# A fused attention and expert kernel: k's copies on ACT, and one batch's choice of experts put behind another's norm

## The chip, the cores and the metric

The kernel runs on one core of a Trainium2 chip. The metric is the device time of one execution in microseconds (us). The engines are PE (TensorE: matrix products and transposes), DVE (VectorE), ACT (ScalarE), POOL (GpSimd) and SP (SyncE, which here only issues DMAs). Each engine has a queue of its own that it works off in order; a semaphore wait at its head holds everything behind it.

## What is computed

Two layers with residuals on x, which is 4 batches of 512 tokens of 256 numbers, all in 32-bit floats:

```
x = x + attn(layernorm(x)) ; x = x + ffn(layernorm(x))

attn(x):  q = k = elu(x @ Wqk + bqk)            # 16 heads of 16
          v = silu(x @ Wv + bv) ; u = silu(x @ Wu + bu)
          kv = k.T @ v (per head) ; out = q @ kv
          out = layernorm(out, ln_g, ln_b) * u
          return out @ Wo + bo

ffn(x):   logits = x @ gate                     # 8 experts
          two best experts per token, softmax over the two
          h = silu(x @ w0[e]) * (x @ w1[e])     # 256 -> 512
          return sum over the two of weight * (h @ wo[e])
```

## The kernel before

**Attention.** `attention(b)` is a Python generator for one batch. Between its `yield`s lie twelve stages, which are numbered here from 0:

- 0: first norm (DVE, and L280 on ACT for odd tiles); 1: transposes of the normed x (L292)
- 2: q and k, which are the same array (L317, exp L322, L323, L324)
- 3: v (L346, L351, L358) and, for batches 0 to 2, u (`project`, L334, L338)
- 4: k's rows: PE transposes them into two PSUM banks (L391), and each bank of 128x512 is copied to SBUF (L394)
- 5: kv (L421, masked at L429); 6: out (L442, copied by L446) and, for batch 3, u
- 7: second norm, `layernorm(..., "2")`; 8: its transposes (L292), scale (L457) and product with u (L461)
- 9: output projection (L469), the residual sum (L473) and the store of the sum to the output (L476, issued by ACT)
- 10: choice of experts (L498 to L520): the two best of eight, third norm, exp for the softmax (L516)
- 11: each token's place in its expert's region, by products with constant matrices (L524, L526), then eight indirect DMAs on POOL that write the rows to `xg` in DRAM (L539)

The norm takes statistics (L252, L253) of four tiles, then ten small dependent DVE steps (L255 to L272), then scales the tiles (L284 on DVE, L280 on ACT).

**Order.** The driver loop counts `at` from 0. Batch b runs stage `at - begin[b]`, with `begin = [0, 4, 8, 12]`, and within one `at` later batches come first. So batch 2 (B - 2) has its stages 9, 10 and 11 at 17, 18 and 19, where batch 3 has its stages 5, 6 and 7.

**Experts.** The rows in `xg` are worked on in blocks of 128 of one expert. After batch 1's stage 11, at 16, `plan` finds nine blocks that are full of the rows of batches 0 and 1 already (`early`). Each block is advanced in a pipeline (`advance`): `fetch` (L715, on SP) loads its rows; `turn` transposes them (L726, copied by L729) and copies two of its expert's weights to a fixed place (L741, ACT and DVE); two half layers (L759 or, for blocks shared by two experts, L767) with silu (L843) and product (L778); `finish` (L798), scale (L809) and an indirect DMA on POOL that adds the rows to the output (L819). `ready` holds the blocks, with `None` where an `at` passes without one: the first early block is fetched at 18, the second at 20, and then one at each `at`.

Blocks that need all batches (`last`, `full`, `second`) come behind the early ones, once batch 3's counts are known.

**What else sets the order.** The tiles' framework schedules: the calls' order is a priority, and an instruction that it takes to be ready goes ahead of one that waits, so that the order on an engine is fixed at compile time but is not the program's. PSUM has eight banks, handed out in turn by `bank`. The last eight weights, `w2` (L174, on SP, called for at 21), are loaded into slots of `arena` that held k and token tiles, so each load waits for the slot's last reader; three of them wait for batch 3's L442 and for the transposes L292 of batches 2 and 3.

Of the kernel before, what the change touches and what calls it, by code (L numbers as in the profile page):

```python
# [32 lines left out]
def kernel(  # L33
# [32 lines left out]
    nc = tc.nc  # L66
    B, N, E = x.shape
    NE, _, M = w0.shape
# [9 lines left out]
    EARLY = 2 * N * TOPK // P - NE + 1  # L78
# [17 lines left out]
    def bank(shape, name, n=1):  # L96

        at = (used[0] + used[0] % n) % BANKS
        used[0] = (at + n) % BANKS
        if n == 2:  # L100
            return banks[:, at : at + 2, 0 : shape[2]]
        tile_ = banks[:, at, 0 : math.prod(shape[1:])]
        if len(shape) == 3:
            tile_ = tile_.rearrange("p (a b) -> p a b", a=shape[1])
        return tile_
# [9 lines left out]
    def att(tag):  # L115

        i = turns[tag] % COUNT[tag]
        turns[tag] += 1
        if tag == "kv":
            return arena[:, AT[tag], bass.ts(i, E)]  # L120
        return arena[:, AT[tag] + i, :]
# [50 lines left out]
    def load_w2():  # L172
        for e in range(NE):
            nc.sync.dma_start(  # L174
                out=arena[:, e, :].rearrange("p (c d) -> p c d", c=MC),
                in_=w2[e].rearrange("(c p) d -> p c d", p=P),
            )
# [121 lines left out]
    def attention(b):  # L299
# [14 lines left out]
        for c in range(EC):  # L314
            ps = bank([P, N], f"qp_{b}_{c}")
            for k in range(EC):
                nc.tensor.matmul(  # L317
                    ps, lhsT=wqk_sb[:, k, bass.ts(c, P)], rhs=xT[:, k, :],
# [23 lines left out]
        for t0 in range(0, NT, 2):  # L342
            ps = bank([P, 2, E + NE], f"vp_{b}_{t0}", 2)
# [18 lines left out]
        if b == 0:  # L362

            ps = bank([P, NE], "gate_sum")
            for k in range(EC):
                nc.tensor.matmul(
                    ps, lhsT=ones, rhs=wv_sb[:, k, E:], start=(k == 0), stop=(k == EC - 1)
# [9 lines left out]
            ps = bank([P, EC, E], "woTp")  # L377
# [8 lines left out]
        kn = att("tok").rearrange("p (t e) -> p t e", t=NT)  # L386
        for t0 in range(0, NT, 2):
            ps = bank([P, 2, E], f"knp_{b}_{t0}")
            for t in range(t0, t0 + 2):
                for c in range(EC):  # L390
                    nc.tensor.transpose(  # L391
                        ps[:, t - t0, bass.ts(c, P)], kT[:, c, bass.ts(t, P)], ident
                    )
            nc.vector.tensor_copy(kn[:, t0 : t0 + 2, :], ps)  # L394
        if b == 0:

            ps = bank([P, EC + 1, NE], "wog")
# [18 lines left out]
        ps = bank([P, EC, HALF], f"kvp_{b}")  # L416
# [21 lines left out]
        for t0 in range(0, NT, 2):  # L438
            ps = bank([P, 2, E], f"op_{b}_{t0}")
# [25 lines left out]
        for t0 in range(0, NT, 2):  # L465
            ps = bank([P, 2, E + NE], f"ap_{b}_{t0}", 2)
# [26 lines left out]
        ps = x1[:, :, E:]  # L493
# [35 lines left out]
        at = small.tile(four, F32, tag="at", name=f"at_{b}")  # L529
# [15 lines left out]
    def total():  # L545

        tot = bank([P, NE], "tot")
        nc.tensor.matmul(tot, lhsT=ones, rhs=state["count"], start=True, stop=True)
        return tot
# [33 lines left out]
    def tmp(shape, what, name):  # L583
        return small.tile(shape, F32, tag=what, name=f"{what}_{name}", bufs=1)

    def upto_each(new, name):

        sq = tmp([1, NE, NE], "sq", name)
        nc.vector.tensor_tensor(
            sq, new.unsqueeze(1).to_broadcast([1, NE, NE]), upto[0:1], ALU.mult  # L590
        )
        cum = tmp([1, NE], "cum", name)
        nc.vector.tensor_reduce(cum, sq, AX.X, ALU.add)
        return cum

    def listed(cum, base, n, name):


        nc.vector.tensor_tensor(
            step[:, 0 : NE - 1], base[:, 1:NE], base[:, 0 : NE - 1], ALU.subtract  # L600
        )

        grid = [1, n, NE]
        behind = tmp(grid, "behind", name)
        nc.vector.tensor_tensor(
            behind, ordinal[:, 0:n, :], cum.unsqueeze(1).to_broadcast(grid), ALU.is_ge
        )
        which = tmp([1, n], "which", name)
        nc.vector.tensor_reduce(which, behind, AX.X, ALU.add)
        nc.vector.tensor_tensor(  # L610
            behind, behind, step.unsqueeze(1).to_broadcast(grid), ALU.mult
        )
        first = tmp([1, n], "first", name)
        nc.vector.tensor_reduce(first, behind, AX.X, ALU.add)
        nc.vector.scalar_tensor_tensor(
            first, first, base[:, 0:1], rows[:, 0:n], ALU.add, ALU.add
        )
        table = const.tile([1, 2, n], I32, name=f"table_{name}")
        nc.vector.tensor_scalar(table[:, 0, :], first, float(NE * REG), None, ALU.min)
        nc.vector.tensor_scalar(table[:, 1, :], which, float(NE - 1), float(OW), ALU.min, ALU.mult)  # L620
        return table
# [36 lines left out]
    def plan(tot, n, b, name):  # L658

        vec = [1, NE]
        c = tmp(vec, "c", name)
        nc.vector.tensor_tensor(c, tot[0:1, :], region[0:1], ALU.subtract)
        full = [1, NE, T // P]
        over = tmp(full, "over", name)
        nc.vector.tensor_tensor(
            over, c.unsqueeze(2).to_broadcast(full), ends, ALU.is_ge
        )
        new = tmp(vec, "new", name)  # L670
        nc.vector.tensor_reduce(new, over, AX.X, ALU.add)
        if b == B - 1:
            nc.vector.tensor_tensor(new, new, done, ALU.subtract)

        cum = upto_each(new, name)
        cumex = tmp(vec, "cumex", name)
        nc.vector.tensor_tensor(cumex, cum, new, ALU.subtract)

        base = tmp(vec, "base", name)
        if b == B - 1:  # L680
            nc.vector.tensor_tensor(base, done, cumex, ALU.subtract)
            nc.vector.scalar_tensor_tensor(base, base, float(P), region[0:1], ALU.mult, ALU.add)
        else:
            nc.vector.scalar_tensor_tensor(base, cumex, -float(P), region[0:1], ALU.mult, ALU.add)
        table = listed(cum, base, n, name)
        if b == B - 1:
            state["found"] = const.tile([1, 1], I32, name="found")
            state["cum"] = const.tile(vec, F32, name="cum_full")
            nc.vector.tensor_copy(state["cum"], cum)
        else:  # L690
            nc.vector.tensor_scalar(done, cumex, -1.0, float(n), ALU.mult, ALU.add)
            nc.vector.scalar_tensor_tensor(done, done, 0.0, new, ALU.max, ALU.min)
        return [
            (f"{name}_{j}", b, None, [table[0:1, 0, j : j + 1]], [table[0:1, 1, j : j + 1]])
            for j in range(n)
        ]
# [160 lines left out]
    STAGES = 12  # L857
    W2_AT = 9
    begin = [0, 4, 8, 12]
    running = [attention(b) for b in range(B)]  # L860
    ready = []
    for at in range(max(begin) + STAGES + 1):
        for b in reversed(range(B)):
            if begin[b] <= at < begin[b] + STAGES:
                next(running[b], None)
        if at == begin[B - 1] + W2_AT:
            load_w2()


        if at == begin[1] + STAGES:  # L870
            blocks = plan(total(), EARLY, 1, "early")
            ready = [None] * 2 + blocks[:1] + [None] * 1 + blocks[1:]
        if at == begin[B - 1] + STAGES:
            tot = const.tile([1, NE], F32, name="tot")
            nc.vector.tensor_copy(tot, total()[0:1, :])
            last, first, end, few = last_rows(tot)
        if ready:
            block = ready.pop(0)
            if block:
                advance(block)  # L880
# [4 lines left out]
    blocks = plan(tot, FULL - EARLY, B - 1, "full")  # L885
# [14 lines left out]
    with tc.If(many > USUAL - EARLY):  # L900
# [7 lines left out]
        for name, some in (  # L908
# [8 lines left out]
            for b in range(B):  # L917
# [3 lines left out]
                at = []  # L921
# [6 lines left out]
                for t in range(NT):  # L928
                    ps = bank([P, E], f"spread_{name}_{b}_{t}")
                    for k in range(NT):  # L930
                        nc.tensor.matmul(
                            ps, lhsT=at[k][:, bass.ts(t, P)], rhs=state["made"][:, k, :],
# [49 lines left out]
```

## Time and profile before

| | us |
|---|---|
| median of 3 runs | 327.46 (326.52 to 327.50) |
| profiled execution, its own time | 326.6 |
| its span, first to last instruction | 324.8 |
| PE busy in the span | 293.6 |
| DVE busy | 157.0 |
| ACT busy | 127.1 |
| POOL busy | 121.7 |

The mean granted clock of PE is 0.964. The page's 40 slices are 8.12 us each; a digit is the busy share in tenths. In a timeline a row is: start, duration, engine, line, operation, out<-in, shape and type, count, and in brackets the idle time before it and what ended it. In the chain of waits a piece is: start, duration, engine or kind, tile, line and count; a merged row can begin earlier in the one view than in the other by some hundredths. A 32-bit product is two instructions on PE, so L469's 16 instructions are 8 products.

### The profile page before, as it was taken

Reading aid. Unit: us, or ns where it says so; the run is one execution under the profiler, and the core shown is the slowest. Engines: PE = TensorE matmul, PEld = TensorE weight load, DVE = VectorE, ACT = ScalarE, POOL = GpSimd, SP = SyncE. Lnnn points to the kernel's source line nnn. Section 1 sums busy time; section 2 is a strip of 40 time slices with the busy share of each in tenths; the row PEclk is TensorE's granted clock in tenths of the full one; section 3 lists DMA queues with packets and bytes.
Section 4 is the critical chain, followed back from the end, with each engine's and each line's share of the span. In section 5 each row is a group of like instructions: output and inputs, shape, how many; then the busy total and the mean of one; then the engine's idle time right before and its main releaser. Section 6 shows DMA issues by size and latency. Waiting matters only on the chain.

```text
span 324.8 us, 5819 instructions
## 1 busy us (share of the span) xinstructions
PE 293.6 (90%) x1948; PEld 235.9 (73%) x1948; DVE 157.0 (48%) x567; ACT 127.1 (39%) x203; POOL 121.7 (37%) x161
## 2 busy tenths in 40 slices
PE   0999999899794599999999999999999999999970
PEld 0567677576663389899974456758999999999960
DVE  5653979979968466843221232332232323233320
ACT  2465566357341835524212144334242424343200
POOL 5340041176461553752331343323343224332321
PEclk9999999999996579999999999999999999999996
DMA  6999403054168450734433122232323433322121
GB/s 199 329 387 385 174 2 109 22 163 163 36 227 266 123 197 9 225 83 64 68 52 54 18 34 35 33 44 33 59 29 63 60 55 61 58 33 34 18 34 20
DMA packets 27731, 32.98 MB, mean 102 GB/s; under 512 B 3249, under 2 KB 22577, under 8 KB 27697
## 3 DMA queue, kind: packets, MB, share of 16 engines
q1 hardware_dynamic: 19056, 21.73, 21.4%
q0 software_dynamic: 6528, 8.72, 16.3%
q10 hardware_dynamic: 2112, 2.10, 1.9%
q8 instruction: 18, 0.29, 0.4%
q14 instruction: 17, 0.13, 0.1%
HBM read 20.53 MB, written 12.01 MB: 100 GB/s over the span
## 4 chain that ended last, share of the span: by engine, by line
PE 73%; DVE 19%; ACT 3%; issue 1%; DMA 1%; POOL 0%; POOLq 0%; DVEq 0%; ACTq 0%
PE banks L759 28%; PE banks L798 19%; PE banks L767 7%; PE banks L469 4%; DVE st L252 4%; PE banks L317 3%; PE banks L726 3%; PE banks L292 2%; PE banks L346 2%; DVE x L473 1%; PE banks L334 1%; PE banks L421 1%; PE banks L785 1%; DVE mv L253 1%; ACT arena L457 1%
## 5 line engine op out<-in xcount | busy, mean ns | idle before, releaser
L759 PE MATMUL banks<-arena 128*128 128x128 f32 x896 | 108.8, 275 | 0.1
L759 PEld LDWEIGHTS banks<-arena 128*128 128x128 f32 x896 | 106.2, 192 | 1.6 <-ACT arena L741 0.3
L729 ACT COPY arena<-banks 128x256 f32<-128x256 f32 x34 | 12.6, 372 | 102.7 <-PE banks L726 102.7
L819 POOL DMA_INDIRECT out_dram<-ys_full,g_full x19 | 30.0, 1577 | 59.5 <-issue 25.7
L539 POOL DMA_INDIRECT xg<-hn,idx_i x32 | 32.0, 999 | 16.9 <-issue 8.5
L798 PE MATMUL banks<-arena,it_full 128*128 x152 | 36.3, 381 | 0.9 <-DVE it_full L778 0.9
L741 ACT COPY arena<-w_sb 128x1024 f32 x30 | 31.3, 1046 | 3.0 <-DVE arena L461 0.8
L798 PEld LDWEIGHTS banks<-arena,it_full 128*128 128x128 f32 x152 | 27.4, 190 | 5.6 <-issue 1.6
L809 DVE TENSOR_SCALAR ys_full<-banks,g_full 128x256 f32<-128x256 f32 x19 | 9.2, 483 | 46.1 <-PE banks L798 46.1
L778 DVE TENSOR_TENSOR it_full<-s_full,banks 128x512 f32<-128x512 f32 x19 | 13.1, 688 | 29.9 <-PE banks L759 29.9
L767 PE MATMUL banks<-w_sb,arena 128*64 128x512 f32 (+1 forms) x80 | 23.2, 605 | 0.0
L819 POOL DMA_INDIRECT out_dram<-ys_early,g_early x9 | 14.1, 1563 | 22.3 <-issue 6.7
L741 DVE COPY arena<-w_sb 128x1024 f32 x30 | 21.4, 712 | 0.9 <-DVE arena L461 0.5
L292 PE MATMUL banks<-ident,arena 128*128 128x128 f32 x64 | 11.2, 317 | 10.5 <-DVE arena L284 8.4
L469 PE MATMUL banks<-wo,arena 128*128 128x264 f32 x64 | 17.5, 434 | 1.4 <-DVE arena L461 1.4
L819 POOL DMA_INDIRECT out_dram<-ys_last,g_last x8 | 11.7, 1463 | 16.9 <-issue 7.9
L798 PE MATMUL banks<-arena,it_early 128*128 x72 | 17.3, 384 | 0.6 <-DVE it_early L778 0.6
L292 PEld LDWEIGHTS banks<-ident,arena 128*128 128x128 f32 x64 | 8.3, 162 | 12.4 <-issue 8.2
L305 POOL TENSOR_TENSOR x<-x,bo 128x256 f32<-128x256 f32 x16 | 12.5, 813 | 12.9 <-DVE arena L284 12.9
L469 PEld LDWEIGHTS banks<-wo,arena 128*128 128x128 f32 x64 | 13.4, 217 | 4.5 <-DVE arena L461 1.8
L317 PE MATMUL banks<-arena,wqk 128*128 128x512 f32 x32 | 16.2, 652 | 0.0
L346 PE MATMUL banks<-wv,arena 128*128 128x264 f32 x64 | 15.7, 397 | 0.0
(212 smaller groups left out, 417.2 us busy)
## 6 DMA issues: line engine op xcount, KB each, us to landing
w_sb<-in_w_dram SPq DMA_DIRECT2D x16, 512.0 KB, 10.8
arena<-in_w_dram SPq DMA_DIRECT2D x8, 512.0 KB, 5.2
g_full<-xg SPq DMA_DIRECT2D x19, 130.0 KB, 2.1
out_dram<-x ACTq DMA_DIRECT2D x4, 512.0 KB, 3.1
x<-in_x_dram SPq DMA_DIRECT2D x3, 512.0 KB, 5.7
xg<-empty SPq DMA_DIRECT2D x9, 130.0 KB, 3.7
g_early<-xg SPq DMA_DIRECT2D x9, 130.0 KB, 3.6
g_last<-xg SPq DMA_DIRECT2D x8, 65.0 KB, 2.1
```

Source lines behind the costliest of these rows:

```text
L252: nc.vector.bn_stats(out=st, in_=src[:, t, :])
L292: nc.tensor.transpose(ps[:, bass.ts(t, P)], src[:, t, bass.ts(c, P)], ident)
L317: nc.tensor.matmul(ps, lhsT=wqk_sb[:, k, bass.ts(c, P)], rhs=xT[:, k, :], start=(k == 0), stop=(k == EC - 1),)
L346: nc.tensor.matmul(ps[:, t - t0, :], lhsT=xT[:, k, bass.ts(t, P)], rhs=wv_sb[:, k, :], start=(k == 0), stop=(k == EC - 1),)
L469: nc.tensor.matmul(ps[:, t - t0, :], lhsT=yT[:, c, bass.ts(t, P)], rhs=wo_sb[:, c, :], start=(c == 0), stop=(c == EC - 1),)
L539: apart(nc.gpsimd.indirect_dma_start(out=xg[:, :], out_offset=bass.IndirectOffsetOnAxis(ap=idx_i[:, t, k : k + 1], axis=0), in_=hn[:, t, k ...
L741: copy(w[i][0], hidden_w2[i][:, bass.ds(at, OW)])
L759: nc.tensor.matmul(ps[:, m, :], lhsT=t[:, bass.ds(at + k * M + m * P, P)], rhs=gT[:, k, :], start=(k == 0), stop=(k == EC - 1),)
L767: nc.tensor.matmul(ps.rearrange("p m n -> p (m n)")[here, :], lhsT=gT[:, k, here], rhs=t[:, bass.ds(at + k * M, M)], start=(k == 0), stop= ...
L778: nc.vector.tensor_tensor(it, s, ps, ALU.mult)
L798: nc.tensor.matmul(ps[here, :], lhsT=it[:, m, here], rhs=t[:, bass.ds(at + m * E, E)], start=(m == 0), stop=(m == MC - 1), tile_position=N ...
L819: ins = nc.gpsimd.indirect_dma_start(out=whole[:, :], out_offset=bass.IndirectOffsetOnAxis(ap=g[0 : P // len(w), E + 1 + u : E + 2 + u].bi ...
```

## The change

Three edits:

1. In stage 4 the copy of k's rows out of the bank (L394) is issued on ACT instead of DVE, for every batch.
2. A table `other` says how often batch 2 (B - 2) is stepped at 17, 19, 20 and 21: not at 17 and 19, once at 20 and 21. So its stage 9 (output projection) is called at 18 instead of 17, its stage 10 (choice) at 20 instead of 18, and its stage 11 (places and scatters) at 21 instead of 19. In each of these `at` batch 3's step is called ahead of it: its out and u at 18, its product with u (stage 8) at 20, its output projection at 21; its second norm at 19 is alone.
3. `ready` starts with three `None`, and then holds all nine early blocks in a row: the first is fetched at 19 instead of 18, the others when they were.

```diff
-            nc.vector.tensor_copy(kn[:, t0 : t0 + 2, :], ps)
+            nc.scalar.copy(kn[:, t0 : t0 + 2, :], ps)
...
     begin = [0, 4, 8, 12]
+
+    other = {17: 0, 19: 0, 20: 1, 21: 1}
     running = [attention(b) for b in range(B)]
     ready = []
     for at in range(max(begin) + STAGES + 1):
         for b in reversed(range(B)):
-            if begin[b] <= at < begin[b] + STAGES:
+            n = int(begin[b] <= at < begin[b] + STAGES)
+            for _ in range(other.get(at, n) if b == B - 2 else n):
                 next(running[b], None)
...
         if at == begin[1] + STAGES:
-            blocks = plan(total(), EARLY, 1, "early")
-            ready = [None] * 2 + blocks[:1] + [None] * 1 + blocks[1:]
+            ready += [None] * 3 + plan(total(), EARLY, 1, "early")
```

## The prediction, made before the changed kernel had run

> **What bounds the kernel now.** I read the page's 40 slices first, then PE's timeline and PE's waits over 75 to 130 us, then the chain of waits over 84 to 119 us, then DVE's and SP's timelines at the points that these named.
>
> ```profile
> PE   0999999899794599999999999999999999999970
> ...
> PEclk9999999999996579999999999999999999999996
> ```
>
> PE is the spine: busy in nine tenths or more almost everywhere. The dip is in slices 11 to 14 (8.1 us each, from 89 us on), and there alone the granted clock falls to half. So the question is what the change does to that stretch. PE's timeline in it (start, duration, work, and in brackets the idle time before it):
>
> ```profile
> 92.84 3.73 PE L469 MATMUL banks<-wo,arena 128*128 128x264 f32 x16
> 96.41 0.83 PE L442 MATMUL banks<-arena 128*128 128x128 f32 x6
> 99.94 0.64 PE L726 MATMUL banks<-ident,g_early 128*128 128x128 f32 x2 [2.71 <-DVE st L252]
> 100.38 0.47 PE L524 MATMUL banks<-mask,earlier 128*128 128x32 f32 x2
> 100.66 1.85 PE L526 MATMUL banks<-mask,ones 128*128 128x32 f32 x8
> 104.50 1.09 PE L726 MATMUL banks<-ident,g_early 128*128 128x128 f32 x4 [1.98 <-DMA g_early<-xg]
> 106.05 0.69 PE L726 MATMUL banks<-ident,g_early 128*128 128x128 f32 x2 [0.46 <-ACT arena L729]
> 106.63 0.69 PE L292 MATMUL banks<-ident,arena 128*128 128x128 f32 x2
> 109.15 1.54 PE L292 MATMUL banks<-ident,arena 128*128 128x128 f32 x6 [1.84 <-ACT arena L280]
> 112.08 6.26 PE L469 MATMUL banks<-wo,arena 128*128 128x264 f32 x16 [1.38 <-DVE arena L461]
> 118.17 5.74 PE L759 MATMUL banks<-arena 128*128 128x128 f32 x50
> ```
>
> The first L469 row is batch 2's output projection, the second batch 3's: the same sixteen instructions take 3.73 us and then 6.26 us, at half clock. From 118.17 on PE runs the experts' blocks with hardly a hole until 315 us. What the reader is to see: batch 3's o (L442) is finished only behind batch 2's projection, and batch 3's norm, transposes and projection, behind which the experts begin, come 15 us after that. The chain of waits says why:
>
> ```profile
> 99.94 0.64 PE banks L726 x2
> 100.59 0.27 PE banks L524 x2
> 100.85 1.68 PE banks L526 x8
> 102.72 0.13 DVE nt L269
> ...
> 107.11 1.28 ACT L516
> 108.40 0.20 ACT two L516
> 108.61 0.50 ACT arena L280
> ```
>
> The PE work that counts batch 2's choices (L524, L526) stands behind the turn of an expert block whose rows have not landed; DVE's queue waits for the counts (L530, idle 1.38 us, ended by L526), and behind it stand the steps of batch 3's second norm. Then ACT's exp of batch 2's choice (L516, a 1.28 us table load and 0.20 us) stands in front of the last two L280, which finish batch 3's norm. Batch 2's choice thus holds up batch 3 on PE, DVE and ACT, and batch 3 is what the experts wait for.
>
> **The change, part by part.** All sums are against the profiled execution: span 324.8 us, its own time 326.6 (1.8 around the span). The median of the runs is 327.46, 0.9 above it; I put the sum on the median.
>
> (a) The five waits of PE above go with their cause: 2.71 + 1.98 + 0.46 + 1.84 + 1.38 = 8.4 us, **-8.4**. What comes in their place is under (d) and (e).
>
> (b) The clock. In stretches of one us it is 1.00 until 99, 0.50 from 100 to 117, and 1.00 again from 118. Work at half clock against the same work at full clock: projection 6.26 against 3.73, 2.5; batch 3's transposes 0.69 + 1.54 against 1.09 (batch 2's, 90.32), 1.1; counting 0.47 + 1.85 against 0.41 + 1.04 (81.24), 0.9; four turns 0.64 + 1.09 + 0.69 against 4 x 0.42 (128.74), 0.7. Together 5.2; I take all of it, **-5.2**, and price its return as a rival. The drop came behind the hole of 2.71 us; holes up to 0.93 us (84.50) caused none.
>
> [...]
>
> (c) k's rows: eight copies of 128x512 leave DVE (L394, median 680 ns, 5.4 us in all) and go to ACT, whose copy of the same shape out of a bank (L446) takes 586 ns, 4.7 us in all. Where DVE is the bound this shortens the chain: L394 stands on it at 85.65 and 86.30 (0.57 and 0.59 us), and DVE is busy for 5.00 of 5 us in 60-65 and 80-85 and 4.99 in 85-90, while ACT has 1.51, 2.94 and 1.22. There PE idles 1.26 us (63.98 to 67.73) and 1.85 us (84.50 to 92.52), 3.1 us that it could win at most. At batch 1's copies (41.26) ACT is busy for 3.99 of 5 us: two copies there bring it to 5.2, a loss of up to 0.6 if PE's next work waits. Batch 0's (24.40) lie beside a DVE that is idle for 2.57 us behind them: nothing. Between +0.6 and -3.1; I take half of the gain, **-1.5**, since PE has other work in most of these stretches. If ACT were full there, each copy would cost its 0.59 us.
>
> (d) New waits. Batch 3 still has to go through norm, transposes, scaling, product, projection, one behind the other. Once batch 2's projection (3.6 us) has covered the norm's statistics and steps, PE waits between batch 3's transposes and its projection as it does now, 1.38 us, and between half-finished norm and transposes, now 1.84 us behind the exp; without exp some 0.5. **+1.9**, between 0.5 and 3.2.
>
> (e) The first block's rows. Its fetch is issued at 97.46, when batch 1's last scatter (POOL, 94.95, 0.97 us) has landed; nothing in the change moves that by more than (c). Rows take 2.3 to 4.5 us to land, so the turn is at 99.9 at the earliest. By my walk batch 3's projection, started as batch 2's ends near 95 plus transposes 1.1 and (d), runs from about 97 to 101, so the rows come just in time; if PE's queue has the turn ahead of the projection, PE waits as it does now, 2.71. **+1.2**, between 0 and 2.7. The loads of the last weights (512 KB each, 3.4 to 5.3 us) get out of the way: of the three that SP now issues at 98.87, 101.61 and 110.77, between the fetches, two wait for batch 3's L442 and batch 2's transposes, both done by 91, and the third for batch 3's transposes, so they move up with these. The fetch queued one step later in the program costs nothing, as the landing of the scatters sets it.
>
> (f) What is put off. Batch 2's choice is 7.7 us of DVE (the rows of L498 to L535 for it added up), two ACT passes, an exp with its tables, and eight scatters on POOL of 1.285 us start to start. Its count and scatters, 10.3 us on POOL, now run beside the experts' blocks, as batch 3's do already (POOL 130.29 to 140.5). Batch 3's rows are first needed by the turn at 162.68, fetched from 144.77: about 20 us of cover, of which the earlier start takes 11 and batch 2's scatters can take most of the rest; nothing for POOL, but no more than that. DVE is tighter: two choices (15.4) and three blocks (0.70 + 0.69 + 0.48 each, 5.6) make 21 us for the first 21 us after batch 3's transposes. PE has up to three half layers (1.79 each) to run while a product is late. Between 0 and 7.7, nearest to 0, as the 120-130 stretch with one choice has DVE at 7.04 of 10 and PE at 9.82: **+1.5**.
>
> Sum: -8.4 - 5.2 - 1.5 + 1.9 + 1.2 + 1.5 = -10.5. Span 314.3, its time 316.1, and on the median 327.5 - 10.5 = **317.0 us**.
>
> **Rivals.**
>
> *The clock falls all the same.* Transposes, a wait, more transposes and a wait remain, some 3 us thinly filled. For: one hole of 2.7 us was enough. Against: 40.37 to 42.6 is transposes alone with a hole of 0.25 us, at clock 1.00. It takes back (b): 317.0 + 5.2 = 322.2. [...]
>
> *The rows are the bound.* PE's queue holds the turns ahead of batch 3's projection, and rows behind each other's fetch cost both holes of now, 4.7 instead of 1.2: 320.5. For: exactly this order stands there now at 99.94 and 104.50. Against: in the new program the projection's inputs are ready earlier, and DMA's load of 0.98 in 100 to 104 moves away.
>
> *DVE is the bound of the first blocks.* Batch 2's choice lies bare: 7.7 instead of 1.5, 323.2.
>
> *Slower.* One place: DVE's queue between batch 3's product (L461) and the first block's copy of w1 (L741). If both choices are queued ahead of this copy, PE has nothing to run but one half layer, and 15.4 us lie bare instead of 1.5: 317.0 + 13.9 = 330.9. It decides as soon as the bare part is above 12 us. Against it: now the first block's product (L778, 123.35) stands in the midst of batch 3's choice.
>
> *It does not do what it says.* The queues don't follow the program's order: batch 3's u (L334) starts at 84.50, before its kv (L421) at 87.03, though the code has them the other way round. If batch 2's steps are drawn forward again, only (c) is left: 326.
>
> **How the numbers follow.** Forecast 0.40 (own range 313 to 319.5: (c), (e) and (f) at their ends), still faster 0.05 (all of (c), none of (e) and (f): 312), clock 0.17, rows 0.15, DVE 0.10, no effect 0.05 and slower 0.08. The range 311.5 to 323.5 takes all faster cases but some tails, 0.82. A measurement of this kernel tells about 0.3%, 1 us, from no change: faster 0.86, same 0.06 (some of "no effect" and the best of "slower"), slower 0.08.
>
> **What would show it.** (a): L442's sixteen in one run before batch 2's L469, batch 3's L292 before any L530 of batch 2, no hole above 2 us. (b): PEclk 9 in slices 12 to 14, and both L469 groups at 3.7 us. (c): copies of k on ACT at 0.59 us, L421 of batch 3 ending before 87 us. (e): the first L726 at about 99 to 100. (f): DVE near 1.0 in the 20 us from the first L759, PE holes behind L778 below 2 us. The sum: first L759 at 101 to 104 instead of 118.17. The prediction is wrong if that row stays above 110, or if it comes early and the blocks behind it wait.

## The result, and the profile after

The changed kernel takes 323.69 us (median of 20 runs, 319.91 to 329.97), the kernel before on the same chip 325.99 us (20 runs, 325.14 to 327.5). The ratio is **0.9905**, interval 0.9884 to 0.9925: 3.1 us faster, where 10.5 were forecast. The ratio leaves out four runs of the changed kernel that took over 1.5% more than its quickest; the quotient of the two medians is 0.9929. The profiled execution of the changed kernel took 320.71 us with a span of 319.0; against the span of 324.8 before, the two profiles differ by 5.8 us. It is the third quickest of the 20; what makes the others some 3 us longer no profile of this chip shows.

The 40 slices of the profile after, PE's share and the granted clock (8.0 us each):

```profile
PE   0999989999698979999999999999999999999930
...
PEclk9999999999989999999999999999999999999995
```

The dip of slices 11 to 14 is filled to seven tenths or more, and the half clock of 17 us is gone. A short half clock is left at slice 11. PE's timeline (start, duration, work, idle time before it and what ended it) shows the new order:

```profile
83.06 1.07 PE L391 MATMUL banks<-ident,arena 128*128 128x128 f32 x8
...
86.31 0.52 PE L421 MATMUL banks<-arena 128*64 128x64 f32 x8 [2.05 <-ACT arena L394]
...
91.97 1.95 PE L442 MATMUL banks<-arena 128*128 128x128 f32 x16
...
95.48 3.72 PE L469 MATMUL banks<-wo,arena 128*128 128x264 f32 x16
99.75 1.41 PE L292 MATMUL banks<-ident,arena 128*128 128x128 f32 x8 [0.54 <-DVE arena L284]
102.03 0.44 PE L726 MATMUL banks<-ident,g_early 128*128 128x128 f32 x2 [0.87 <-DMA g_early<-xg]
102.39 2.05 PE L469 MATMUL banks<-wo,arena 128*128 128x264 f32 x8
...
108.30 3.74 PE L759 MATMUL banks<-arena 128*128 128x128 f32 x32
...
115.36 3.81 PE L759 MATMUL banks<-arena 128*128 128x128 f32 x32 [2.15 <-DVE hn L520]
```

Batch 3's out (L442) now runs in one piece ahead of batch 2's projection (L469 at 95.48), batch 3's projection at full clock from 102.39, and the first expert block starts at 108.30 instead of 118.17. That is 9.9 us earlier, yet the kernel ends only 5.8 us earlier. PE's last product ends 8.4 us earlier (306.95, 315.39 before). The rest is lost behind PE. POOL's timeline after:

```profile
124.49 1.41 POOL L511 COPY hn<-hn 128x256 f32<-128x256 f32 x4
126.07 0.99 POOL L539 DMA_INDIRECT xg<-hn,idx_i  x1 [0.17 <-issue]
...
135.41 0.97 POOL L539 DMA_INDIRECT xg<-hn,idx_i  x1 [0.31 <-issue]
136.69 1.60 POOL L819 DMA_INDIRECT out_dram<-ys_early,g_early  x1 [0.30 <-DVE new_second L637]
141.30 1.58 POOL L819 DMA_INDIRECT out_dram<-ys_early,g_early  x1 [3.02 <-issue]
...
305.70 1.54 POOL L819 DMA_INDIRECT out_dram<-ys_full,g_full  x1 [2.93 <-DVE it_full L778]
310.35 1.55 POOL L819 DMA_INDIRECT out_dram<-ys_full,g_full  x1 [3.11 <-issue]
```

and the same places in the profile before:

```profile
127.24 1.60 POOL L819 DMA_INDIRECT out_dram<-ys_early,g_early  x1 [0.53 <-issue]
130.29 1.22 POOL L539 DMA_INDIRECT xg<-hn,idx_i  x1 [1.44 <-DVE idx_i L533]
...
140.79 1.64 POOL L819 DMA_INDIRECT out_dram<-ys_early,g_early  x1 [0.30 <-issue]
...
311.56 1.54 POOL L819 DMA_INDIRECT out_dram<-ys_full,g_full  x1 [3.75 <-DVE ys_full L809]
316.19 1.55 POOL L819 DMA_INDIRECT out_dram<-ys_full,g_full  x1 [3.09 <-DVE ys_full L809]
```

L819 adds a block's rows to the output. There are 40 such adds, and each waits until the one before has landed (3.1 to 4.3 us from issue to landing in the profile after): 1.55 us of issue and some 3 us of idle, start to start 4.45 us on the mean ((310.35 - 136.69) / 39). Before, the first add went out at 127.24, ahead of batch 3's scatters, the second behind them at 140.79, and by the end each add waited for its block (DVE's L809). After, batch 2's eight scatters stand at 114.35 to 124.5, batch 3's at 126.07 to 136.4, and the first add behind both, 9.5 us later than before. But the second add stands behind batch 3's scatters in both kernels, and it comes only 0.5 us later (141.30). So the chain of adds has hardly moved, while PE's end has come 8.4 us forward, and now the chain ends last: the last add starts 3.4 us behind PE's last product (0.8 before), and the span ends 12.0 us behind it (9.4 before).

### The profile page after: what moved, and what is told of

Its sections match the earlier page's. It is cut to its first block, busy times and chain, and to the rows that moved or that the text cites. A ratio compares the mean times of both kernels' runs of the same rounds, so it can differ in the third digit from the quotient of the medians.

```text
span 319.0 us, 5814 instructions
## 1 busy us (share of the span) xinstructions
PE 289.6 (91%) x1948; PEld 232.7 (73%) x1948; DVE 150.6 (47%) x559; ACT 128.5 (40%) x209; POOL 121.8 (38%) x161
## 5 line engine op out<-in xcount | busy, mean ns | idle before, releaser
L759 PE MATMUL banks<-arena 128*128 128x128 f32 x896 | 108.8, 275 | 2.3 <-DVE hn L520 2.1
L759 PEld LDWEIGHTS banks<-arena 128*128 128x128 f32 x896 | 106.0, 192 | 3.9 <-issue 2.3
L819 POOL DMA_INDIRECT out_dram<-ys_full,g_full x19 | 30.1, 1582 | 55.9 <-issue 29.5
L741 ACT COPY arena<-w_sb 128x1024 f32 x30 | 31.3, 1046 | 2.9 <-ACT arena L729 1.0
L809 DVE TENSOR_SCALAR ys_full<-banks,g_full 128x256 f32<-128x256 f32 x19 | 9.2, 484 | 46.2 <-PE banks L798 46.2
L819 POOL DMA_INDIRECT out_dram<-ys_early,g_early x9 | 14.0, 1553 | 25.7 <-issue 16.1
L767 PE MATMUL banks<-w_sb,arena 128*64 128x512 f32 (+1 forms) x80 | 23.2, 605 | 0.0
L741 DVE COPY arena<-w_sb 128x1024 f32 x30 | 21.2, 706 | 3.1 <-PE banks L759 1.5
L292 PE MATMUL banks<-ident,arena 128*128 128x128 f32 x64 | 10.3, 300 | 9.3 <-DVE arena L284 9.0
L798 PE MATMUL banks<-arena,it_early 128*128 x72 | 17.1, 381 | 0.0
L819 POOL DMA_INDIRECT out_dram<-ys_last,g_last x8 | 11.9, 1493 | 12.6 <-issue 5.5
L305 POOL TENSOR_TENSOR x<-x,bo 128x256 f32<-128x256 f32 x16 | 11.6, 754 | 11.8 <-DMA bo<-in_bo_dram 7.8
L469 PE MATMUL banks<-wo,arena 128*128 128x264 f32 x64 | 15.4, 391 | 0.8 <-DVE arena L461 0.8
L334 PE MATMUL banks<-arena,wu 128*128 128x512 f32 x32 | 15.9, 630 | 0.0
L292 PEld LDWEIGHTS banks<-ident,arena 128*128 128x128 f32 x64 | 7.7, 152 | 11.1 <-issue 9.6
```

The lines of the kernel that those rows point to most:

```text
L292: nc.tensor.transpose(ps[:, bass.ts(t, P)], src[:, t, bass.ts(c, P)], ident)
L334: nc.tensor.matmul(ps, lhsT=wu_sb[:, k, bass.ts(c, P)], rhs=xT[:, k, :], start=(k == 0), stop=(k == EC - 1),)
L469: nc.tensor.matmul(ps[:, t - t0, :], lhsT=yT[:, c, bass.ts(t, P)], rhs=wo_sb[:, c, :], start=(c == 0), stop=(c == EC - 1),)
L741: copy(w[i][0], hidden_w2[i][:, bass.ds(at, OW)])
L759: nc.tensor.matmul(ps[:, m, :], lhsT=t[:, bass.ds(at + k * M + m * P, P)], rhs=gT[:, k, :], start=(k == 0), stop=(k == EC - 1),)
L767: nc.tensor.matmul(ps.rearrange("p m n -> p (m n)")[here, :], lhsT=gT[:, k, here], rhs=t[:, bass.ds(at + k * M, M)], start=(k == 0), stop= ...
```

## The experiments

Theory A: POOL's chain of 40 adds sets the end of the changed kernel. Theory B: PE does, as before. The chips drawn for the experiments differ from the first one: the kernel before takes 339 to 341 us on all four of them and 326 us on the first. So only ratios within one chip are compared.

| run | edit | chip | ratio to before | interval |
|---|---|---|---|---|
| after_again | none | 8 | 0.9864 | 0.9814 to 0.9914 |
| copy_only | before, k's copies on ACT | 8 | 1.0039 | 1.0004 to 1.0075 |
| order_only | after, k's copies on DVE | 8 | 0.9824 | 0.9768 to 0.9881 |
| no_early_adds | after, nine adds out | 8 | 0.9760 | 0.9705 to 0.9815 |
| before_no_adds | before, nine adds out | 10 | 0.9997 | 0.9963 to 1.0031 |
| adds_first | after, first add ahead of scatters | 10 | 0.9904 | 0.9864 to 0.9943 |
| u_banks | after, banks of u | 10 | 1.0117 | 1.0051 to 1.0184 |
| all_three | after, copies + banks + first add | 10 | 1.0193 | 1.0129 to 1.0257 |
| before_look | none, before | 0 | 1.0029 | 0.9990 to 1.0068 |
| after_look | none | 0 | 0.9826 | 0.9770 to 0.9881 |
| adds_first_2 | as adds_first | 0 | 0.9913 | 0.9872 to 0.9954 |
| order_adds | after, copies + first add | 0 | 0.9824 | 0.9768 to 0.9880 |
| after_third | none | 6 | 0.9779 | 0.9730 to 0.9828 |
| adds_first_3 | as adds_first | 6 | 0.9877 | 0.9816 to 0.9937 |
| three_adds | after, two adds more | 6 | 0.9886 | 0.9820 to 0.9953 |
| double_b2 | after, eight scatters more | 6 | 1.0178 | 1.0119 to 1.0237 |

### The parts of the change, one by one

The change once more, and its two parts alone:

> The changed kernel once more, for a second profile and for the spread of its runs. Theory A (the adds' chain sets the end): POOL's 40 indirect adds to the output follow one another without a gap that PE causes, from the end of batch 3's last scatter to the end, 4.4 to 4.6 us each; the last product on PE ends some 12 us before the span does, where it is 9.4 in the kernel before; ratio to before 0.985 to 0.995 and a spread of several us among runs. Theory B (PE sets the end): PE's last product ends 9.4 us before the span does, and a run that is longer is longer on PE.

> The kernel before with k's copies on ACT and nothing else. By the prediction's term (c): 1.5 us faster than before (ratio 0.9954), between 3.1 us faster and 0.6 slower. By the reading of the changed kernel's profile: no gain, since ACT's queue holds batch 3's copies behind the silu of v, which waits for DVE, and batch 1's behind two passes of a norm: between 0 and 2 us slower (ratio 1.000 to 1.006).

> The changed kernel with k's copies back on DVE: batch 2's later steps and the later first block alone. If the copies on ACT gain what the prediction's term (c) says, this is 1.5 us slower than the changed kernel (ratio to before 0.995). If they cost something on PE but the adds' chain sets the end (theory A), the chain's start decides: within 1.5 us of the changed kernel (0.986 to 0.995). If they cost on PE and PE sets the end (theory B): 1 to 4 us faster than the changed kernel (0.978 to 0.987).

```
-            nc.scalar.copy(kn[:, t0 : t0 + 2, :], ps)
+            nc.vector.tensor_copy(kn[:, t0 : t0 + 2, :], ps)
```

(The diff of order_only against the changed kernel; copy_only is the reverse on the kernel before.) The gain is in the order of the batches. The copies on ACT bring nothing: alone they are 0.4% slower, which is little more than the kernel before differs from itself (before_look, 1.0029), and with DVE's copies the new order is 0.4% faster than with ACT's, the intervals overlapping. That pair does not compare the copies alone, as the compiled order of POOL differs too: in order_only the first add goes out at 131.09, ahead of batch 3's scatters, and the second at 144.14. Nor does the start of the blocks decide the end on this chip: order_only's first L759 comes 5.3 us later than after_again's (120.31 against 115.03), and its PE still ends 1.0 us earlier (324.02 against 325.00). The profiles show what the copies do. With the new order, PE idles 2.05 us ahead of batch 3's kv with ACT's copies (2.06 in after_again), and 2.80 us with DVE's, as this line of order_only's PE timeline shows; so there ACT's copies do shorten the wait:

```profile
86.72 0.45 PE L421 MATMUL banks<-arena 128*64 128x64 f32 x8 [2.80 <-DVE var L255]
```

But the same copies make a new hole of 0.80 us at batch 1's (45.37 in the first profile after; copy_only has it too, before and order_only don't), and batch 3's L391 comes 0.7 us later (83.06, before 82.38).

### The adds

The nine adds of the early blocks taken out of the changed kernel, then out of the kernel before:

```
+        if b < B - 1:
+            return
         for u in range(len(w)):
```

> The changed kernel without the adds of the nine early blocks' results to the output: their products are computed and scaled, and not added. Theory A: the chain of the other 31 adds starts late enough to wait for PE at the end, so the span ends some 9.4 us behind PE's last product, which stays at about 307: span 316 to 317, 2.5 to 3 us less than the changed kernel's profile, ratio to before about 0.970 to 0.976, and the runs lie within 2 us of each other. Theory B: no change against the changed kernel, 0.985 to 0.995.

> The kernel before without the adds to the output of the nine early blocks (their share of the output is left out; the other 31 adds stay). It is the control for the run that left the same nine adds out of the changed kernel and took 1.1% off it. Theory A (in the changed kernel POOL's chain of 40 adds sets the end; before, the chain had caught up with the blocks by the end): nothing to gain here, ratio 0.997 to 1.003, tail from PE's last product to the end of the span 9 to 9.5 us as before. Rival B (the nine adds cost time in any kernel, by their load on the DMA engines or on POOL): 1.1% faster here too, ratio about 0.989.

Without them the changed kernel gains 1.1% on the run beside it, the kernel before nothing. That agrees with A, but does not carry it: on this chip the changed kernel's last add started 0.8 us behind PE's last product (325.80 and 325.00), so the chain was not its bound there, and PE itself ended 3.2 us earlier without the adds (321.8), which A does not account for. Next, the first add was queued ahead of batch 3's scatters:

```
+        with tc.issue_after(state["add"]) if b == B - 1 else nullcontext():
             for t in range(NT):
...
             tc.add_to_no_dep_group("adds", ins.ins)
+            state["add"] = ins.ins
```

> The changed kernel, with the first early block's add queued on POOL ahead of batch 3's eight scatters instead of behind them; nothing else moves on any engine. Theory A: the first add is issued at about 124.5 us instead of 136.7, the chain stands one interval (4.45 us) further ahead, the last add waits for its block again, the tail behind PE's last product falls from 12.0 to 9.0-9.5 us, and the time falls by some 2.5 us against the changed kernel: ratio to before 0.975 to 0.983. Theory B (PE sets the end): as the changed kernel, ratio 0.986 to 0.9905, and 1.5 us more if batch 3's rows come late for it.

> The changed kernel with the first add ahead of batch 3's scatters, beside the changed kernel itself. Theory A: where the changed kernel has the tail of 12 us, 2.5 us (0.8%) faster than it; where its tail is 9.5 us already, the same within 0.4%. Theory B (PE alone sets the end): the same in both cases.

> The changed kernel with the first add ahead of batch 3's scatters. On a chip of the first sort, theory A (POOL's chain of adds sets the end there): 2.5 us or more faster than the changed kernel, tail 9.5 us; theory B: the same. On one of the slow sort both theories expect what the two runs before showed, 0.990 to 0.991, since the first add waits for a block that PE's hole made late, and holds up batch 3's scatters by some 7 us.

On chip 10 the ratio lies at the upper edge of theory B's range, but the twelve runs lie between 331.74 and 340.81 us and no run of the changed kernel stands beside them, so this decides little. On chip 0 both theories missed: the edit is 0.9% slower than the changed kernel beside it. On chip 6 it is 1.0% slower, as by then expected. In after_look and after_third the last add starts 0.8 us behind PE's last product, so there is nothing to win; and the first add waits for its block's result and holds the scatters. POOL's timeline of adds_first_3:

```profile
131.44 1.42 POOL L511 COPY hn<-hn 128x256 f32<-128x256 f32 x4
137.19 1.60 POOL L820 DMA_INDIRECT out_dram<-ys_early,g_early  x1 [4.33 <-DVE ys_early L810]
139.09 1.02 POOL L540 DMA_INDIRECT xg<-hn,idx_i  x1 [0.30 <-issue]
```

The scatters start at 139.09, 7.5 us later than in after_third (131.6). No chip with the 12 us tail was drawn, so whether this order wins there was not tried. The test that tells A from B on any chip is to lengthen the chain alone:

```
+            for _ in range(3 if j == "early_0" else 1):
                 ins = nc.gpsimd.indirect_dma_start(
                     out=whole[:, :],
...
```

> The changed kernel beside the next three. On a chip of the first sort (before at 326 us): ratio 0.988 to 0.993, last add 3 us behind PE's last product, tail 12 us. On one of the slow sort (before at 340 us): 0.980 to 0.988, holes of PE of 2 to 4 us at 119 to 145 us, last add some 0.8 us behind PE's last product.

> The changed kernel with the first early block's add issued three times (its share of the output is then counted three times): two more links in POOL's chain, and no work for PE. Theory A: the chain ends at its first add + 41 x 4.5 us; on a chip of the first sort it is the bound already, so the time grows by 9 us (+2.8% on the changed kernel); on one of the slow sort, where the chain has some 3 us of slack, by some 6 us (+1.8%). Theory B (PE sets the end in both): no change, under 0.4%.

By the two ratios it takes 1.1% or 3.6 us more than the changed kernel beside it, where A expected 6 and B under 1.3. The two intervals still touch (0.9820 and 0.9828), so the times alone don't decide it, and the profiles have to. PE's and POOL's last rows, first of after_third, then of three_adds:

```profile
321.59 1.99 PE L798 MATMUL banks<-arena,it_full 128*128 x8 [0.85 <-DVE it_full L778]
```

```profile
324.38 1.55 POOL L819 DMA_INDIRECT out_dram<-ys_full,g_full  x1 [3.09 <-DVE ys_full L809]
```

```profile
320.81 1.99 PE L798 MATMUL banks<-arena,it_full 128*128 x8 [0.85 <-DVE it_full L778]
```

```profile
321.79 1.54 POOL L820 DMA_INDIRECT out_dram<-ys_full,g_full  x1 [2.95 <-issue]
326.36 1.55 POOL L820 DMA_INDIRECT out_dram<-ys_full,g_full  x1 [3.03 <-issue]
```

In after_third the last add waits for its block; in three_adds no block's result is named any more, the idle time is the 3 us that each add waits for the one before, and the last add starts 3.6 us behind PE's last product, although PE ends earlier (322.8 against 323.6). That is the picture of the first profile after. So A holds as a rule: the last add starts at the later of two times, 0.8 us behind PE's last product, or the start of the chain + its links x 4.5 us (143.40 + 41 x 4.46 in three_adds). For the changed kernel the second is later on the first chip, and the first on the three others on which it ran.

### Banks, and everything together

Batch 3's u (L334) takes, after the change, the same two PSUM banks as batch 3's k rows, so PE can't run it while these are copied. Giving u other banks:

```
+        ups = [bank([P, N], f"up_{b}_{c}") for c in range(EC)] if b >= LATE else None
         for t0 in range(0, NT, 2):
             ps = bank([P, 2, E], f"op_{b}_{t0}")
...
-                ps = bank([P, N], f"up_{b}_{c}")
+                ps = ups[c] if ups else bank([P, N], f"up_{b}_{c}")
```

> The changed kernel, with the two PSUM banks of batch 3's u taken ahead of those of batch 3's out, so that u no longer shares the banks of k's rows and can run on PE beside k's copies. Theory A says the 2.05 us hole ahead of batch 3's kv (84.25 to 86.31) and the half clock from 86.6 to 90.0 come from PE having nothing else to run there: the hole falls below 1 us, no half clock at 86 to 90, first product of an expert block at 104 to 106 instead of 108.3, and ratio 0.980 to 0.986 if the adds' chain, which starts behind batch 3's scatters, moves up with them. Rival D (the copies of k on ACT themselves are what is late, whatever PE has to run): the hole stays near 2 us and the ratio at 0.986 to 0.9905.

> The changed order of the batches with k's copies back on DVE, u's own banks and the first add ahead of batch 3's scatters. If the three causes are separate, their shares add up: 0.4% (copies), 0.8% (adds), 0.8% (banks) off the changed kernel, ratio to before 0.966 to 0.974. If the adds' chain is the only bound of the end (theory A alone), banks and copies bring nothing on top: 0.975 to 0.983. If PE alone sets the end (theory B), the add's place brings nothing: 0.975 to 0.980, with a tail of 9 to 9.5 us in every case.

> The same with k's copies back on DVE: the two edits that the runs so far speak for, without u's banks. If the copies on ACT cost time (0.4% in the first set): ratio 0.4% below the run before it, 0.974 to 0.982 on either sort of chip. If they cost nothing: the same as that run within 0.3%.

PE's timeline of u_banks at that place:

```profile
86.29 3.39 PE L334 MATMUL banks<-arena,wu 128*128 128x512 f32 x4 [1.00 <-DVE x L354]
89.61 1.15 PE L421 MATMUL banks<-arena 128*64 128x64 f32 x32
```

The hole fell to 1.00 us as expected, but u fills it from ahead of kv, and kv is done at 90.76, no earlier than without the edit (89.83 in adds_first on the same chip, 90.21 in the first profile after). So nothing is won for the chain behind kv. The half clock, which was expected to go, stayed (granted clock 0.5 from 85.7 to 89.2), and the first expert block comes at 119.6, not at 104 to 106. u_banks is 2.1% slower than adds_first beside it; the two profiles differ by 12.4 us. Half of that is there by the first L759 (119.6 against 113.3 us). The holes of PE between 92 and 110 us explain little of that (7.2 us in sum, in adds_first 5.7), but in u_banks batch 3's out, counting and projection run at half clock behind them: 3.29, 1.85 and 5.96 us instead of 2.05, 1.04 and 4.00. Most of the rest is two holes of 5.1 and 6.3 us at 127 and 146 us, where adds_first has one of 2.5 at 128 us. Their cause is open (below), and all_three has the like. The shares did not add up. order_adds is as fast as the plain change on its chip, 0.9% faster than adds_first_2, and no complete version that was tried beats the new order alone beyond its interval.

### The holes of the four other chips

The kernel before and after on one chip:

> The kernel before once more, for a profile on the same chip as the next three: ratio 1 within 0.3%. If a chip of the slow sort (around 340 us) is drawn, theory S says that its extra time is in holes of PE while batches of row scatters are under way, because PE's releases come late there: holes of 2 to 7 us between 90 and 150 us that the first profile (326 us) did not have. If a chip of the first sort is drawn: PE's holes behind 118 us below 1 us, and POOL's last add some 0.8 us behind PE's last product.

> The changed kernel once more, beside the next two. Ratio 0.984 to 0.992. Theory A (POOL's chain of 40 adds sets the end where the blocks run without holes): on a chip of the first sort, last add 3 us or more behind PE's last product and a tail of 12 us; on a chip of the slow sort, where PE ends some 15 us later, last add about 0.8 us behind PE's last product and a tail of 9 to 9.5 us.

The expectation of before_look calls it theory S that PE's holes come from the row scatters. That there are holes of 2 to 7 us held. PE's timeline of before_look:

```profile
138.90 2.39 PE L759 MATMUL banks<-arena 128*128 128x128 f32 x20
148.39 3.78 PE L798 MATMUL banks<-arena,it_early 128*128 x8 [7.10 <-DVE it_early L778]
```

The first profile before has no hole above 0.40 us there. From the first L767 on all profiles need the same time to PE's last product (146.9 us: 168.5 to 315.4 in the first profile before, 182.7 to 329.6 here); all that PE loses on these chips, it loses before that. In before_look and after_look the span falls from 339.0 to 330.1 us, 8.9 us, and the last add starts 0.8 us behind PE in both: where the chain of adds is not the bound, the whole gain of PE's end arrives. To see whether the holes come from the scatters that are under way then, batch 2's were doubled, into an array that nobody reads:

```
+        for t in range(NT if b == B - 2 else 0):
+            for k in range(TOPK):
+                ins = nc.gpsimd.indirect_dma_start(
+                    out=xh[:, :], out_offset=bass.IndirectOffsetOnAxis(ap=idx_i[:, t, k : k + 1], axis=0),
...
```

> The changed kernel with batch 2's eight row scatters followed by eight more of the same rows to a second array that nobody reads: POOL's batch lasts some 20 us instead of 10, and batch 3's scatters and the adds come 10 us later. Theory S (on chips of the slow sort PE's releases stay away until the packets of the scatters under way have drained): PE's hole that now ends with batch 2's scatters, near 131 us, ends with the longer batch, near 139 to 142 us, and is 7 us or more longer in sum. Rival T (the holes belong to PE's own work or clock at that point of the program): the hole stays at 128 to 132 us with 2 to 4 us, and only the end of the kernel moves, by up to 10 us through the chain of adds. On a chip of the first sort, where no such hole is seen, both expect none.

PE's rows of after_third and of double_b2 (its lines lie 9 further down):

```profile
132.11 2.08 PE L759 MATMUL banks<-arena 128*128 128x128 f32 x8 [3.95 <-DVE arena L741]
...
145.30 3.39 PE L798 MATMUL banks<-arena,it_early 128*128 x8 [2.09 <-DVE it_early L778]
```

```profile
132.24 1.90 PE L768 MATMUL banks<-arena 128*128 128x128 f32 x8 [3.93 <-DVE arena L750]
...
142.78 1.01 PE L807 MATMUL banks<-arena,it_early 128*128 x2 [1.05 <-issue]
...
156.53 3.58 PE L807 MATMUL banks<-arena,it_early 128*128 x8 [4.75 <-DVE it_early L787]
```

Batch 2's scatters last until 130.0 in the one and 140.7 in the other, and this hole is the same: theory S falls for it. But rival T does not stand either. From 136 to 157 us (POOL issues scatters up to 154) double_b2 has nine holes above 0.3 us with 9.6 us in sum, where after_third has one of 2.1. In most of them the profile names nothing that PE waits for. With the hole at 132 they come to 13.5 us against 6.0, the "7 us or more" that S named. The kernel is 4.1% slower than after_third (two runs), and PE's last product comes 11.1 us later with the last add 0.8 us behind it, so the loss is on PE and not, as T has it, in the chain of adds. More scatters cost PE time on this chip; by what path was not found, nor what makes the hole at 132 us.

## Why the prediction was wrong

The direction, the new order and the place of the gain were right; the size was not. On the first chip's two profiles the terms come out so (the sum was made against the span):

| term | forecast | measured | from |
|---|---|---|---|
| (a), (c), (d), (e): PE's holes between 40 us and the first L759 | -6.8 | -6.4 | 12.0 us before, 5.6 after |
| (b): the clock | -5.2 | -3.5 | 17.1 us of half clock gone (-5.2); 3.4 us new, half of it lost (+1.7) |
| start of the first L759 (the two rows above) | -12.0 | -9.9 | 118.17 to 108.30 |
| (f): the blocks behind it, DVE | +1.5 | +1.4 | PE's end -8.4 |
| (f): POOL | 0 | +2.6 | tail 9.4 to 12.0 |
| span | -10.5 | -5.8 | 324.8 to 319.0 |

**The step that failed** is in (f): "nothing for POOL, but no more than that". It asked only when batch 3's rows are needed, and there it was right (the turn of the first such block came at 154.25, without a wait on them). It did not ask what stands behind the scatters in POOL's queue: 40 adds, each waiting for the landing of the one before. The profile before had the numbers. Its second add went out at 140.79, behind batch 3's scatters, and 38 links of 4.45 us from there end at 309.9, so the chain stood only 6.3 us ahead of the last add at 316.19, whose block came late. A forecast of 10.5 us needed more room than that, or batch 3's scatters done earlier; and by (f)'s own numbers batch 3's earlier start (11 us) and batch 2's scatters ahead of its own (10.3 us) all but cancel. The change moves the chain back by 0.5 us (141.30) and leaves 5.8 us, which is what the span won; PE's end came 8.4 us forward, and the 2.6 us between them are the longer tail. POOL was busy for 37% of the span, and that figure hid a queue which is full in another sense, one add in flight at a time. three_adds shows the rule on another chip; the 2.6 us themselves are read from the first chip's profiles alone, and no run on that chip moved the chain by itself. Rival "slower" named an engine's queue between two steps, but DVE's, not this one; at its place there is the hole of 2.15 us, not 13.9.

**(a)** held: the five waits are gone with their cause. **(b)** held for the 17 us, but behind the 2.05 us hole at k's rows half clock came back for 3.4 us; u_banks has it there behind a hole of 1.00 us too, so the reading that holes up to 0.93 us cost no clock does not give a rule. **(c)** was taken as -1.5 and is about nothing: 0.97 us fewer of holes at batch 2's copies and 0.80 more at batch 1's, and alone 0.4% slower, not faster. At batch 3's copies 2.05 us stand in the place of 0.93, as the order takes u away as PE's filler, and kv ends at 90.21 where the sign asked for 87. **(d)** cost less than its 1.9: 0.54 us between norm and transposes, and between transposes and projection PE waits only for the first block's rows, which (e) counts. **(e)** was right in price, 0.87 us, by luck: the turn came at 102.03 instead of 99.9, as batch 1's last scatter was issued 1.0 us later (95.91) and the fetch behind it 2.4 us later (99.83), where (e) allowed no more than (c); batch 3's projection came late as well. **(f)** on DVE was right: 1.4 us, with the hole of 2.15 us at 113.21, where the copy of w1 (L741 at 114.52) stands behind steps of both choices. The signs given for the first L759 (101 to 104) were tighter than the terms themselves, which come to 106.2.

Of the difference between 5.8 us in the profiles and 3.1 us in the ratio no run shows the cause. On the three other chips on which the changed kernel ran, the change is worth 1.4 to 2.2%, 4.6 to 7.5 us.

## What to carry to other kernels

An engine at 38% busy can be the bound, as POOL in the profile after, if its instructions wait for each other's landing, there 4.45 us from start to start: count such a chain as start plus links times interval, and ask of each step that is moved onto that queue what it pushes back. When a gain on the critical path is forecast, work out when the next path ends, too, counting its links from where they really run without a break: here it had 6 us of room for a gain that was forecast at 10. And a hole is worth closing only with work that the chain behind it doesn't have to wait for: u in front of kv closed one and won nothing.

## What was not expected of the hardware

**Half clock lasted 3.41 us or a multiple of it, and the length of a hole did not decide it.** The stretches of the profile after (from and to, length, PE, PEld, DVE, ACT and POOL busy with their instructions, granted clock, DMA share, GB/s), cut at the borders of its half clock and at multiples of 3.41 us from there:

```profile
83.20:86.60 3.40, 1.35 (x19) 1.26 (x17) 3.40 (x20) 2.08 (x4) 0.35 (x2) 0.99 0.00 0
86.60:90.00 3.40, 3.40 (x32) 1.78 (x28) 3.26 (x27) 1.23 (x3) 2.58 (x3) 0.50 0.21 76
...
110.50:113.90 3.40, 2.71 (x25) 2.52 (x23) 3.17 (x20) 2.44 (x5) 1.59 (x4) 1.00 0.32 114
113.90:117.30 3.40, 1.94 (x17) 1.97 (x18) 2.88 (x14) 2.06 (x3) 2.34 (x3) 1.00 0.12 42
117.30:120.70 3.40, 3.40 (x33) 3.40 (x32) 1.30 (x6) 3.37 (x6) 2.66 (x3) 1.00 0.35 122
```

The hole of 2.05 us lies inside one of these stretches, PE is busy for 1.35 us of it, and the next one runs at half clock. The longer hole of 2.15 us lies across two (2.71 and 1.94 us busy) and costs no clock. Between 15 us and PE's last product, half clock lasts 3.41 us in the profile after (86.56 to 89.97) and 17.07 us, five times as long, in the profile before (99.97 to 117.03). Behind 40 us it lasts about 3.4, 6.8 or 13.6 us each time in after_again, copy_only, order_only and no_early_adds. PE's busy time in a stretch does not settle it alone. Cut in the same way, the profile before has 0.71 us of work from 96.55 to 99.97 and half clock behind it, and then, at half clock, 2.55, 1.83, 1.58 and 2.03 us, each with half clock behind it again; 2.48 us at 82.90 has none behind it, nor has 1.94 us here, while 2.57 us in u_banks, at 82.3, has.

**A release of PE came 4.1 us after its product was issued.** In after_third a product issued at 127.21 gives its semaphore at 131.34, by the trace's semaphore events; in the first profile after the distance is 0.29 us (120.01 to 120.30). DVE and ACT then wait for PE, and PE for them: DVE's copy of w1 (L741) starts at 131.36, after 6.95 us of idle, and PE's next product at 132.11, after 3.95. The chips around 340 us show holes with it in both kernels (in before_look a product issued at 140.79 and a semaphore at 147.59); in the first chip's profile after no release is later than 1.2 us. The cause stays open: doubling batch 2's scatters left the hole of after_third as it was and brought others behind it.

**An accumulating indirect DMA of 128 rows cost some 4.5 us in the chain** (147.03 to 151.49 in the profile after), 1.54 us of it on POOL. Each add waits here for the one before, and no run tried without that wait.
